# Four casts of two bias rows, made by ScalarE instead of VectorE

## The chip, the cores and the metric

The kernel runs on one core of a Trainium2 chip. The metric is the device time of one execution in microseconds (us), the median of several runs. The engines are TensorE (PE, and PEld for its weight loads), VectorE (DVE), ScalarE (ACT), GpSimd (POOL) and SyncE (SP, which issues most of the DMAs).

## The reference, cut to what matters

The input is four images of 64 x 64 positions with 96 channels. Two layers follow one another. The first normalizes each image, projects every position and runs a gated linear recurrence with 96 x 16 states along the 4096 positions of an image; it is most of the work. The second is attention without softmax and a feed forward layer whose numbers are rounded to small float formats:

```python
# q_mul rounds to fp8 (5 exponent bits, 2 mantissa bits), q_acc to fp16 (5, 10)
def _qlinear(x, W, b):
    y = q_acc(jnp.einsum('bsk,nk->bsn', q_mul(x), q_mul(W)))
    return q_acc(y + q_mul(b))
h = jax.nn.relu(_qlinear(x, W1, b1))     # 96 -> 384
y = _qlinear(h, W2, b2)                  # 384 -> 96
```

So the two biases, b1 of 384 numbers and b2 of 96, are rounded to fp8 once and then added as they are.

## The kernel before, in words

An image is cut into 8 chunks of 512 positions, 32 chunks in all. A chunk's recurrence is 12 tiles of 128 states by 512 positions, so there are K = 384 tiles, and the program is one loop over steps s from 0 to 383. In each step the engines get, in this order of issue: on TensorE the B matmuls of tile s + 3 (`b_proj`), the A matmuls of tile s + 1 (`a_proj`) and the C matmuls of tile s (`c_proj`), three each, all by the helper `project` (line 292); on ScalarE the copy of B with its bias into the buffer bu (`b_copy`, line 924) and the copy of the last state (`keep`, line 953); on GpSimd the product of bu of tile s + 2 (`b_mul`, line 927) and, for some tiles, the product of C (`c_mul_pool`, line 976); on VectorE the scan of tile s (`scan`, line 943), the product of A of tile s + 1 (`a_mul`, line 936), and for the other tiles the product of C (`c_mul`, line 967).

What is not part of a tile's own work is put behind that, at `call(s)`, from a table of steps written by hand: the projections of the next chunk, its norms, the sums over states, the attention and the feed forward layer of earlier chunks. Each engine works through its instructions in the order in which they were issued. The first steps and the part behind step 383 are ordered by a planner (`Plan`) that goes by the engines' costs that the code states.

PSUM banks: A has two, B one, C and D one each, and M three, which all side work shares in turn. The A bank of a tile is free again when its scan has read it, the B bank when `b_copy` has.

The weights of the second layer are prepared in steps far ahead of their use: `weights_attention`, `weights_ffn1`, `weights_ffn2` and `weights_bias` at steps 20, 32, 44 and 56 transpose them on TensorE, and the step after each writes them out of PSUM. For the biases that is `biases_out` in step 57: b1 from PSUM to fp8 (line 381) and back to f32 (line 382), then b2, loaded in full width by a DMA at the start, from SBUF to fp8 (line 384) and back to f32 (line 385). The readers of the results are `relu` and `relu_vector` (lines 1249 and 1260) and `bias_out` (line 1284), from 379 us on.

Of the kernel before, what the change touches and what calls it, by code (L numbers as in the profile page):

```python
# [13 lines left out]
AF = mybir.ActivationFunctionType  # L14
# [4 lines left out]
B, H, W, C = 4, 64, 64, 96  # L19
# [15 lines left out]
NK = HID // P  # L35
# [21 lines left out]
APPLY_DVE = (2, 6)  # L57
QUANT_POOL = (1, 3, 4, 5)
BIAS_DVE = (0, 2, 3, 4, 5, 7)
TOTAL_DVE = (0, 2, 3, 4, 5)  # L60
ON_POOL = (0, 2, 9)
AT0 = {
# [19 lines left out]
def conv_attn_hybrid_kernel(  # L82
# [19 lines left out]
    nc = tc.nc  # L102
# [21 lines left out]
    def sb(tag, shape, dtype, name):  # L124
        pool = big if tag in ("x", "gx", "z", "rep") else work
        return pool.tile(shape, dtype, tag=tag, name=name, bufs=BUFS[tag])
# [128 lines left out]
    b1_q = const.tile([P, NK], F32, name="b1_q")  # L255
    b2_q = const.tile([P, C], F32, name="b2_q")
# [3 lines left out]
    b2_sb = sb("y16", [P, C], F32, "b2_sb")  # L260
# [113 lines left out]
    def weights_bias():  # L374
        ps = bank("M", [P, NK], "b1_ps")
        nc.tensor.transpose(ps, b1_sb, ident[:NK, :NK])
        return lambda: biases_out(ps)

    def biases_out(ps):
        b1_8 = small.tile([P, NK], F8, tag="b1_8", name="b1_8", bufs=1)  # L380
        nc.vector.tensor_copy(b1_8, ps, saturate=False)
        nc.vector.tensor_copy(b1_q, b1_8)
        b2_8 = small.tile([P, C], F8, tag="b2_8", name="b2_8", bufs=1)
        nc.vector.tensor_copy(b2_8, b2_sb, saturate=False)
        nc.vector.tensor_copy(b2_q, b2_8)

    norms = {}

# [800 lines left out]
    def ffn(b, i, s0):  # L1189
        nm = f"{b}_{i}"  # L1190
        whole = s0 + max(AT["attention"], AT["residual_f"]) >= K
# [3 lines left out]
        v, ln = {}, LayerNorm(1e-5, f"f_{nm}", key)  # L1195
        t = xt[b, i]

        def tile_of(tag, drain_tag, shape, dtype, name):
            return sb(drain_tag if phase["end"] else tag, shape, dtype, f"{name}_{nm}")
# [32 lines left out]

        def quant_in():
            v["xq"] = tile_of("xq", "h", [C, TC], F8, "xq")
            nc.scalar.activation(v["xq"], v["ps"][0:C], AF.Copy, saturate=False)  # L1235

        def hidden(m):
            v["h", m] = bank("M", [P, TC], f"h_ps{m}_{nm}")
# [14 lines left out]
        def round_hidden(m):  # L1253
            if m == 0:
                v["h16"] = sb("rep", [P, NK, TC], F16, f"h16_{nm}")
            nc.scalar.copy(v["h16"][:, m, :], v["h", m])  # L1256

        def relu_vector(m):
            h = v["h16"][:, m, :]
# [32 lines left out]
        def store():  # L1292
# [6 lines left out]
            (("rstd_f", ln.rstd),),  # L1299
            (("apply_f", apply),),  # L1300
            (("transpose_f", transpose), ("quant_in", quant_in)),
            tuple((f"{f.__name__}{m}", f, m) for m in range(NK) for f in (hidden, relu)),
            (("project_f", project_out), ("round_out", round_out)),
# [17 lines left out]
        def job(engine, cost, fn, *args, **kw):  # L1321
            return None if fn in done else end.job(engine, cost, fn, *args, **kw)
# [9 lines left out]
        def finish(a, mv):  # L1332
            end.rank = END_RANKS[1] if b < B - 1 else END_RANKS[2] + END_PAIR[i]
            if vector:
                a = job("DVE", 0.96, apply, after=[a], take=[f"xn8:{nm}"], free=mv, late=0.1, port=True)
            elif whole:
                a = job("ACT", 1.45, apply, after=[a], take=[f"xn8:{nm}"], free=mv, late=0.1)
            if transpose not in done:
                a = job("PE", 0.25, transpose, after=[a], take=[f"C:{nm}"], free=[f"xn8:{nm}"], late=0.2)
                a = job("ACT", 0.49, quant_in, after=[a], take=[f"h:{nm}"], free=[f"C:{nm}"], late=0.1)  # L1340
            if hidden not in done:
                r, h, c = [], None, None
                for m in range(NK):
                    h = job("PE", 0.22, hidden, m, after=[a, h], take=[f"M:{m}{nm}"],
                            free=[f"h:{nm}"] if m == 2 else [], late=0.2)
                    c = job("ACT", 0.48, round_hidden, m, after=[h, c],
                            take=[f"rep:{nm}"] if m == 0 else [], free=[f"M:{m}{nm}"], late=0.1)
                    r.append(job("DVE", 0.27, relu_vector, m, after=[c], late=0.1, port=True))
                if i in QUANT_POOL:
                    a = job("POOL", 1.43, quant, after=r, take=[f"bu:q{nm}"], free=[f"rep:{nm}"], late=0.1, port=True)  # L1350
                else:
                    a = job("ACT", 1.38, quant, after=r, take=[f"bu:q{nm}"], free=[f"rep:{nm}"], late=0.1)
            a = job("PE", 0.5, project_out, after=[a], take=[f"A:y{nm}"], free=[f"bu:q{nm}"], late=0.2)
            a = job("ACT", 0.37, round_out, after=[a],
                    take=[f"xs:{nm}"], free=[f"A:y{nm}"], late=0.1)
            e = "DVE" if whole and i in BIAS_DVE else "POOL"
            a = job(e, 0.55 if e == "DVE" else 0.88, bias_out, e, after=[a], take=[f"xl:{nm}"], free=[f"xs:{nm}"], late=0.1, port=True)
            e = "DVE" if whole and i in TOTAL_DVE else "POOL"
            a = job(e, 0.5 if e == "DVE" else 0.88, total, e, after=[a], take=[f"z:{nm}"], free=[f"xl:{nm}"], late=0.1, port=True)
            job("SP", 0.5, store, after=[a], late=2.5, free=[f"z:{nm}"])  # L1360

        if whole:
            wholes[b, i] = begin, finish, ln
            return
        end.rank = END_RANKS[1]
        a = job("DVE", 0.48, residual)
        a = job("DVE", 1.04, stats, after=[a], take=[f"mv1:{nm}"], late=0.1)
        a = job("POOL", 1.3, ln.rstd, after=[a], late=0.1)
        if apply not in done:
            a = job("ACT", 1.45, apply, after=[a], take=[f"xn8:{nm}"], free=[f"mv1:{nm}"], late=0.1)  # L1370
        finish(a, [])

    wholes = {}
# [275 lines left out]
```

## Time and profile before

| what | value |
|---|---|
| median of 3 runs | 1141.15 us (1138.0 to 1142.48) |
| profiled execution: its own time | 1141.61 us |
| profiled execution: span from first to last instruction | 1139.9 us |
| granted TensorE clock, mean | 0.993 |
| instructions | 20132 |
| busy share: TensorE, VectorE, GpSimd, ScalarE | 96%, 96%, 90%, 79% |
| the four casts | once, from 190.93 to 192.51 us |

In the lines of a profile a group reads: line, engine, operation, output <- inputs by the program's names without numbers (so b1_q and b2_q are both b_q, b1_sb and b2_sb both b_sb, b1_8 and b2_8 just b), and shapes as partitions x elements. In a timeline each line begins with the start and the duration in us; what stands in brackets at its end is the idle time of that engine before it, and what ended that. In a view of waits the three numbers are the total in us, the number of waits and the longest. A release that the view names is the last event by its reckoning; where the engine it names had long been done, it was another.

### The profile page before, as it was taken

To read this page: it belongs to the slowest core of one execution; us is meant where nothing else is said; L and a number is where in the kernel's file an instruction comes from. 1 tells how busy PE (TensorE), PEld (TensorE's weight loads), DVE (VectorE), ACT (ScalarE), POOL (GpSimd) and SP (SyncE) were. 2 spreads that over 40 slices of the span, in tenths; PEclk is the share of its full clock that TensorE was granted. 3 is DMA by queue.
4 is the path that set the end of the run, shared out by engine and by line. 5 is a ranking of instruction groups with operands and counts; after the bars stand their busy time and mean duration, and the time that the engine had idled before them with its cause. 6 is when DMAs were issued, how large, how long until landed. Compare 5 with 4: busy or idle time off the path is not lost. (4 is left out here: it accounts for less than half of the span.)

```text
span 1139.9 us, 20132 instructions
## 1 busy us (share of the span) xinstructions
PE 1097.5 (96%) x5691; PEld 860.8 (76%) x5691; DVE 1089.5 (96%) x1874; ACT 904.5 (79%) x2448; POOL 1029.8 (90%) x1048
## 2 busy tenths in 40 slices
PE   6999999999999999999999999999999999999985
PEld 5677777777877777777778777777777777777663
DVE  6999999999999999999999999999999999999985
ACT  4587666766766988888898889889888888886577
POOL 5688999899999999999999999999999899999754
PEclk8999999999999999999999999999999999999999
DMA  7578988888888988988888888888898888797432
GB/s 185 129 155 166 193 175 167 172 190 174 183 183 170 190 179 177 180 180 188 175 185 191 185 181 184 172 173 186 178 181 181 170 182 178 166 186 165 91 91 56
DMA packets 98074, 193.62 MB, mean 170 GB/s; under 512 B 48509, under 2 KB 56641, under 8 KB 97962
## 3 DMA queue, kind: packets, MB, share of 16 engines
q0 software_dynamic: 17376, 91.63, 44.5%
q1 hardware_dynamic: 79996, 100.69, 35.3%
q8 instruction: 45, 0.74, 0.3%
q14 instruction: 67, 0.55, 0.1%
q10 hardware_dynamic: 590, 0.02, 0.0%
HBM read 20.36 MB, written 12.58 MB: 29 GB/s over the span
## 5 line engine op out<-in xcount | busy, mean ns | idle before, releaser
L927 POOL TENSOR_TENSOR bu<-bu,rep 128x512 f32<-128x512 f32 x384 | 596.0, 1587 | 13.8 <-ACT bu L924 6.5
L943 DVE TENSOR_TENSOR_SCAN h<-Aps,state,bu 128x512 f32<-128x512 f32 x336 | 427.1, 1271 | 7.7 <-POOL bu L927 3.4
L924 ACT ACTIVATE bu<-Bps,b_bac 128x512 f32<-128x512 f32 x384 | 262.8, 684 | 113.2 <-PE Bps L292 105.1
L936 DVE SCALAR_TENSOR_TENSOR Aps<-Aps,b_bac,rep 128x512 f32<-128x512 f32 x384 | 281.6, 734 | 4.5 <-PE Aps L292 4.2
L292 PE MATMUL Bps<-xs,w 128*128 128x512 f32 x768 | 265.7, 427 | 6.8 <-ACT bu L924 6.5
L292 PE MATMUL Aps<-xs,w 128*128 128x512 f32 x768 | 243.2, 397 | 1.4 <-DVE h L943 1.0
L292 PEld LDWEIGHTS Aps<-xs,w 128*128 128x128 f32 x768 | 142.1, 188 | 41.7 <-DVE h L943 9.0
L976 POOL TENSOR_TENSOR ch<-ch,h 128x512 f32<-128x512 f32 x94 | 151.3, 1610 | 3.9 <-ACT ch L973 3.8
L292 PEld LDWEIGHTS Bps<-xs,w 128*128 128x128 f32 x768 | 128.6, 190 | 31.1 <-ACT bu L924 14.2
L292 PE MATMUL Aps<-xl,w 128*128 128x512 f32 x384 | 151.7, 395 | 0.0
L292 PE MATMUL Bps<-xl,w 128*128 128x512 f32 x384 | 151.4, 394 | 0.0
L292 PE MATMUL Cps<-xs,w 128*128 128x512 f32 x384 | 120.6, 395 | 0.0
L292 PE MATMUL Dps<-xs,w 128*128 128x512 f32 x384 | 120.6, 395 | 0.0
L967 DVE SCALAR_TENSOR_TENSOR ch<-Dps,b_bac,h 128x512 f32<-128x512 f32 x161 | 119.3, 741 | 0.4 <-PE Dps L292 0.3
L983 POOL DMA_DIRECT2D ch<-ch x94 | 107.4, 1142 | 7.4 <-DMA ch<-ch 3.2
L967 DVE SCALAR_TENSOR_TENSOR ch<-Cps,b_bac,h 128x512 f32<-128x512 f32 x129 | 95.5, 740 | 0.0
L292 PEld LDWEIGHTS Bps<-xl,w 128*128 128x128 f32 x384 | 72.2, 188 | 17.7
L292 PEld LDWEIGHTS Aps<-xl,w 128*128 128x128 f32 x384 | 72.0, 188 | 17.7
L292 PEld LDWEIGHTS Cps<-xs,w 128*128 128x128 f32 x384 | 72.0, 188 | 17.6
L292 PEld LDWEIGHTS Dps<-xs,w 128*128 128x128 f32 x384 | 72.0, 188 | 17.6
L292 PE MATMUL Dps<-xl,w 128*128 128x512 f32 x192 | 75.7, 394 | 0.0
L292 PE MATMUL Cps<-xl,w 128*128 128x512 f32 x192 | 75.6, 394 | 0.0
(212 smaller groups left out, 2181.3 us busy)
## 6 DMA issues: line engine op xcount, KB each, us to landing
ch<-ch POOLq DMA_DIRECT2D x94, 768.0 KB, 6.7
rep<-dd SPq DMA_DIRECT2D x372, 128.0 KB, 4.0
ch<-ch POOLq DMA_DIRECT2D x30, 384.0 KB, 5.4
xl<-lo SPq DMA_DIRECT2D x62, 128.0 KB, 3.2
x<-in_x_dram SPq DMA_DIRECT2D x32, 192.0 KB, 3.2
xatd<-xat SPq DMA_DIRECT2D x32, 192.0 KB, 2.8
xal<-xatd SPq DMA_DIRECT2D x32, 192.0 KB, 4.4
out_dram<-o SPq DMA_DIRECT2D x32, 192.0 KB, 3.9
```

Source lines behind the costliest of these rows:

```text
L292: nc.tensor.matmul(ps, lhsT=wt[:, n], rhs=mv, start=(n == 0), stop=(n == 2))
L924: nc.scalar.activation(self.bu, self.b_ps, AF.Identity, bias=self.bias(0))
L927: nc.gpsimd.tensor_tensor(self.bu, self.bu, rep[self.b, self.i][:, self.cg, 1], ALU.mult)
L936: nc.vector.scalar_tensor_tensor(self.a_ps, self.a_ps, self.bias(1), rep[self.b, self.i][:, self.cg, 0], ALU.add, ALU.mult,)
L943: nc.vector.tensor_tensor_scan(self.h, self.a_ps, self.bu, 0.0 if self.i == 0 else state[self.sh, self.cg], ALU.mult, ALU.add,)
L967: nc.vector.scalar_tensor_tensor(self.slot(), self.c_ps, self.bias(2), self.h, ALU.add, ALU.mult)
L976: nc.gpsimd.tensor_tensor(self.ch, self.ch, self.h, ALU.mult)
L983: nc.gpsimd.dma_start(chs[g, base(g)], chs.pop((g, sh)), accum_op=ALU.add)
```

## The change

The four casts in `biases_out` are issued to ScalarE, as two activations with the function Copy into fp8 and two copies back to f32. Two tuples, both empty, are added at the top, and two places of the feed forward layer and of its planning ask whether a tile is in them; with the empty tuples they issue what they issued before.

```diff
+QIN_DVE = ()
+ROUND_DVE = ()
...
     def biases_out(ps):
         b1_8 = small.tile([P, NK], F8, tag="b1_8", name="b1_8", bufs=1)
-        nc.vector.tensor_copy(b1_8, ps, saturate=False)
-        nc.vector.tensor_copy(b1_q, b1_8)
+        nc.scalar.activation(b1_8, ps, AF.Copy, saturate=False)
+        nc.scalar.copy(b1_q, b1_8)
         b2_8 = small.tile([P, C], F8, tag="b2_8", name="b2_8", bufs=1)
-        nc.vector.tensor_copy(b2_8, b2_sb, saturate=False)
-        nc.vector.tensor_copy(b2_q, b2_8)
+        nc.scalar.activation(b2_8, b2_sb, AF.Copy, saturate=False)
+        nc.scalar.copy(b2_q, b2_8)
...
         def quant_in():
             v["xq"] = tile_of("xq", "h", [C, TC], F8, "xq")
-            nc.scalar.activation(v["xq"], v["ps"][0:C], AF.Copy, saturate=False)
+            if whole and i in QIN_DVE:
+                nc.vector.tensor_copy(v["xq"], v["ps"][0:C], saturate=False)
+            else:
+                nc.scalar.activation(v["xq"], v["ps"][0:C], AF.Copy, saturate=False)
...
-            nc.scalar.copy(v["h16"][:, m, :], v["h", m])
+            if whole and NK * i + m in ROUND_DVE:
+                nc.vector.tensor_copy(v["h16"][:, m, :], v["h", m])
+            else:
+                nc.scalar.copy(v["h16"][:, m, :], v["h", m])
...
-                a = job("ACT", 0.49, quant_in, after=[a], take=[f"h:{nm}"], free=[f"C:{nm}"], late=0.1)
+                e = "DVE" if whole and i in QIN_DVE else "ACT"
+                a = job(e, 0.6 if e == "DVE" else 0.49, quant_in, after=[a], take=[f"h:{nm}"], free=[f"C:{nm}"], late=0.1)
...
-                    c = job("ACT", 0.48, round_hidden, m, after=[h, c],
+                    e = "DVE" if whole and NK * i + m in ROUND_DVE else "ACT"
+                    c = job(e, 0.6 if e == "DVE" else 0.48, round_hidden, m, after=[h, c],
```

## The prediction

> **What bounds the kernel now.** I read the page from the top: engine shares first, then the 40 slices, then the chain.
>
> ```profile
> PE 1097.5 (96%) x5691; PEld 860.8 (76%) x5691; DVE 1089.5 (96%) x1874; ACT 904.5 (79%) x2448; POOL 1029.8 (90%) x1048
> DVE  6999999999999999999999999999999999999985
> ACT  4587666766766988888898889889888888886577
> ```
>
> VectorE (DVE) is busy 90% or more of nearly every slice, with TensorE (PE) level with it, so time taken from VectorE can count; ScalarE (ACT) has slack in the early slices, where the four casts run. The chain that ended last is of no use here: followed back from the end it covers only the last 65 us, from 1075 us on, and the casts run near 191 us. So the question is local, and I go to the timeline of each engine around the casts. First VectorE (start, duration, line, operation, idle before it in brackets):
>
> ```profile
> 187.67 1.28 DVE L943 TENSOR_TENSOR_SCAN h<-Aps,state,bu 128x512 f32<-128x512 f32 x1
> 189.56 0.76 DVE L936 SCALAR_TENSOR_TENSOR Aps<-Aps,b_bac,rep 128x512 f32<-128x512 f32 x1 [0.61 <-PE Aps L292]
> 190.26 0.75 DVE L967 SCALAR_TENSOR_TENSOR ch<-Dps,b_bac,h 128x512 f32<-128x512 f32 x1
> 190.93 0.15 DVE L381 CAST b<-b_ps 128x3 fp8e5<-128x3 f32 x1
> 191.12 1.13 DVE L382 CAST b_q<-b 128x3 f32<-128x3 fp8e5 x1
> 192.16 0.20 DVE L384 CAST b<-b_sb 128x96 fp8e5<-128x96 f32 x1
> 192.39 0.21 DVE L385 CAST b_q<-b 128x96 f32<-128x96 fp8e5 x1
> 192.51 1.27 DVE L943 TENSOR_TENSOR_SCAN h<-Aps,state,bu 128x512 f32<-128x512 f32 x1
> ```
>
> The reader is to see two things. The casts run once in the whole kernel and take VectorE from 190.93 to 192.51 us, 1.58 us from the end of the multiply to the next scan. And one of them, three elements wide, takes 1.13 us where its like takes 0.15. GpSimd's (POOL's) timeline over the same stretch says why:
>
> ```profile
> 188.77 2.20 POOL L927 TENSOR_TENSOR bu<-bu,rep 128x512 f32<-128x512 f32 x1
> 190.02 2.19 POOL L976 TENSOR_TENSOR ch<-ch,h 128x512 f32<-128x512 f32 x1
> 191.27 1.11 POOL L676 TENSOR_TENSOR gmv<-gt,gmc 96x1 f32<-96x1 f32 x1
> ```
>
> GpSimd's product of line 976 ends at 192.21 and the cast of line 382 at 192.25. Then ScalarE's timeline, where the casts go:
>
> ```profile
> 188.92 0.69 ACT L924 ACTIVATE bu<-Bps,b_bac 128x512 f32<-128x512 f32 x1
> 189.51 0.18 ACT L953 COPY state<-h 128x1 f32<-128x1 f32 x1
> 191.02 0.69 ACT L924 ACTIVATE bu<-Bps,b_bac 128x512 f32<-128x512 f32 x1 [1.33 <-POOL bu L927]
> 191.61 0.18 ACT L953 COPY state<-h 128x1 f32<-128x1 f32 x1
> 193.76 0.69 ACT L924 ACTIVATE bu<-Bps,b_bac 128x512 f32<-128x512 f32 x1 [1.97 <-PE Bps L292]
> ```
>
> ScalarE idles 1.33 us and then 1.97 us. The view names GpSimd for the first gap, but the copy at 191.02 also needs the third B matmul, which ended at 190.92 (start 190.53, 0.39 long): that is what it waited for.
>
> **What the Trainium skill says.** "SBUF — State Buffer", section "Who interferes with whom": VectorE and GpSimd share a port pair under an exclusive lock that is held for a whole instruction; copies and casts from SBUF to SBUF can enter the mode that takes it, and the loser blocks. The trace agrees as far as it can: line 382 (SBUF to SBUF) takes 1.13 us and ends with GpSimd's product, line 381 (from PSUM, as narrow) 0.15. The same section gives ScalarE ports of its own, so I expect no such stall there; no run shows these casts on it. "ScalarE: Activation LUTs", section "What ACT_TABLE_LOAD costs": an ACTIVATE with immediates takes 186 ns + 0.833 ns an element, and neighbours overlap by about 93 ns. The trace's nearest rows are near it: 128x1 copies 182 ns, 128x4 activations with immediates 189 to 206 ns, 97x97 copies from PSUM 232 to 236 ns, 128x96 activations 274 ns. The trace has a single ACT_TABLE_LOAD, of 1283 ns, although Sigmoid, Copy, Identity, Square and Relu follow it, so these casts bring no second one.
>
> **The change part by part.**
>
> *Taken from VectorE: four casts.* Busy 0.15 + 1.13 + 0.20 + 0.21 = 1.69 us; what counts is the pitch, 1.58 us. Can the scan of tile 58 start at 190.93 instead of 192.51? Its A operand is the multiply at 189.56, done by 190.32. Its bu is GpSimd's product of tile 58, started at 186.54 and done by 188.75 (product 59 is issued in step 57, just ahead of the product of C for tile 56, so product 58 is one earlier). Both are there: the whole 1.58 us is exposed on VectorE.
>
> *Can the neighbours follow?* The next A multiply (tile 59) needs matmuls that end at 191.62; VectorE would reach it at 190.93 + 1.19 = 192.12. The C product of tile 58 needs matmuls ending near 192.32; reached at 192.77. The scan of 59 needs bu at 190.97; reached at 193.42. The A multiply of 60 needs an A bank that the scan of 58 frees at about 192.2; TensorE could then issue it at 193.5, when its B matmuls are issued, not at 193.84, and end near 194.4; VectorE comes at 194.61. So no new wait follows in the next steps, and the lead is carried.
>
> *How much of it survives.* In the stretch after the casts the waits of TensorE's weight loads are VectorE's doing:
>
> ```profile
> PEld Aps L292 <- DVE h L943: 3.3, 6, 0.6
> ```
>
> That is the view of waits from 192 to 257 us: six waits, 3.3 us in all. Of them the matmul stream itself loses about 0.34, 0.29, 0.28, 0.2 and 0.2 us by 211 us (each start against the previous start plus the 0.235 us at which unstalled matmuls follow one another), and another 0.34 at 242.5: some 1.3, then 1.65 us, that TensorE can gain once VectorE comes earlier. VectorE's first idle time after the casts is at 247.16 us, 0.17 us, for TensorE's A matmuls. Until then VectorE never waits, so it keeps up to 1.58 us; from there TensorE's lead is what counts, 1.3 to 1.6. Later releasers (GpSimd's bu at 339 us, 0.53; the chain of the gram matrix at 344 us, 1.76 on TensorE) are issued behind the same engines and should come earlier with them, but part may be lost. I take **1.3 us** kept, with 0.2 and 1.6 as the ends.
>
> *Put on ScalarE: four casts.* They come behind the state copy of step 57 (ends 189.69) and ahead of the bu copy at 191.02. Their matmul ran at 186.88 and the bias row was loaded at 43 us, so neither is waited for. Price: two of 3 columns at 0.19 (rows of 128x4), two of 96 at 0.24 to 0.27 (the rows above) = 0.86 to 0.92 us; with the overlaps of the skill 0.64 (estimate); with a pause of 0.19 us ahead of three of them, as the one between the affine and the copy at 194.42 and 195.36, 1.5. The cover is the gap of 1.33 us, so 0 to 0.17 us stick out, and these meet the 1.97 us gap: the bu copy frees the one B bank, whose next matmul starts at 192.71, a full microsecond after it. Cost taken: 0. Without that cover TensorE's B matmuls would be late by whatever is over about 2.3 us.
>
> *Waits that change owner.* The first cast now gives the M bank back from ScalarE, near 189.9 instead of 191.1; its next tenant is the group sum at 192.59. The later readers of the two bias tiles wait for ScalarE instead of VectorE, from 379 us on, nearly 190 us after; nothing is queued behind that. No DMA and no queue of SP or GpSimd moves. GpSimd loses the rival for its port, worth at most its stretched line 676 (1.11 against 0.19 us), beside work that nobody waits for at once. The new branches name two empty tuples: the instructions they issue and the costs the end's planner sees are those of before. Cost 0.
>
> *Sum.* -1.3 + 0 + 0 = -1.3 us, so the profiled execution (1141.61 us, 1.71 of it outside the 1139.9 span) would come to 1140.3. That execution stands 0.46 us above the median of 1141.15, so the median goes to **1139.9 us**: 0.1%. The three runs before spread over 4.5 us, and a measurement of this kernel can tell about 0.5%, 5.7 us, from no change. So the answer is no change that can be told.
>
> **The rivals.**
>
> *The lead is swallowed.* A later wait that isn't VectorE's doing absorbs it. For: TensorE is as full as VectorE (33.00 of 33 us in the stretch from 355 to 388). Against: TensorE's own waits up to 242 us name VectorE. Gives 1141 us. Chance 0.20.
>
> *Slower: the casts delay the B bank.* B has one bank; what the four casts take beyond 2.3 us (the gap and the microsecond behind it) stops TensorE. It decides from 0.58 us a cast, three times the 128x4 row. At 0.75 each, 3.0 us, TensorE would be 0.7 us late and the bu stream behind it, and the lead is gone: 1141.9 us. For: no row shows a copy out of fp8 on ScalarE. Against: copies into fp8 there follow the usual price (598 ns for 512 columns). Chance 0.05.
>
> *Displaced transfers.* DMA engines are 81 to 87% busy in these stretches; 1.5 us of shift can change which transfer runs into which. The longest wait of GpSimd on a DMA is 1.7 us, so one collision costs 0.4 net (1141.6) or brings as much; for 5.7 us it would have to repeat four times or more. Chance 0.12, of which I put 0.10 beyond 0.5%, evenly to both sides.
>
> *The change does nothing*, if VectorE's scan waits at 190.93 for something this profile hides: 1141.15. It lies within the swallowed case.
>
> **How the numbers follow.** Gain kept 0.63, swallowed 0.20, displaced 0.12, slower 0.05. Beyond 0.5% on either side: 0.05 each from displaced transfers, and 0.01 each for a fault in the others. So faster 0.06, within 0.88, slower 0.06. The range takes the kept gain's ends (1139.6 to 1141.0), the slow rival's 1141.9, and the spread of medians that runs of 1138.0 to 1142.5 allow: 1136.9 to 1143.0.
>
> **What would show it.** Right: VectorE's timeline has no cast near 191 and the scan follows the multiply within 0.05 us; ScalarE shows four casts of 0.18 to 0.28 us between a state copy and a bu copy that starts no later than 191.3; the wait of TensorE on line 943 next after it is shorter. VectorE busy falls by some 1.7 us, ScalarE's grows by 0.9. Wrong: a bu copy later than 192, casts over 0.5 us, a table load beside them, or a median more than 5.7 us off.

## The result, and the profile after

| | before | after |
|---|---|---|
| median of 22 runs each | 1141.6 us | 1139.12 us |
| ratio after to before, 95% interval | | 0.998 (0.9973 to 0.9986) |
| profiled execution, span | 1139.9 us | 1135.9 us |

That is 2.3 us less (1.6 to 3.1). The sign is the one forecast, 1139.12 us lies within the range of 1136.9 to 1143.0, and the change is smaller than 0.5%. It is more than the 1.3 us of the sum, and it can be told from no change after all: with 22 runs each the interval leaves 1 out. The page of the changed kernel is nearly the same; VectorE has lost 1.3 us of busy time and four instructions, ScalarE has gained the four:

```profile
PE 1097.0 (97%) x5691; PEld 862.4 (76%) x5691; DVE 1088.2 (96%) x1870; ACT 904.8 (80%) x2452; POOL 1029.3 (91%) x1048
```

VectorE's timeline of the changed kernel at the casts' old place:

```profile
187.81 1.28 DVE L945 TENSOR_TENSOR_SCAN h<-Aps,state,bu 128x512 f32<-128x512 f32 x1
189.71 0.76 DVE L938 SCALAR_TENSOR_TENSOR Aps<-Aps,b_bac,rep 128x512 f32<-128x512 f32 x1 [0.61 <-PE Aps L294]
190.41 0.75 DVE L969 SCALAR_TENSOR_TENSOR ch<-Dps,b_bac,h 128x512 f32<-128x512 f32 x1
191.07 1.27 DVE L945 TENSOR_TENSOR_SCAN h<-Aps,state,bu 128x512 f32<-128x512 f32 x1
...
194.76 0.73 DVE L938 SCALAR_TENSOR_TENSOR Aps<-Aps,b_bac,rep 128x512 f32<-128x512 f32 x1
```

This execution runs 0.15 us later than the one before up to here (189.71 against 189.56). The multiply of line 969 is followed by the scan at once: from one scan to the next it takes 191.07 - 187.81 = 3.26 us, where it took 192.51 - 187.67 = 4.84. That is 1.58 us less, and no idle time opens in the steps that follow. ScalarE's timeline of the changed kernel:

```profile
189.66 0.18 ACT L955 COPY state<-h 128x1 f32<-128x1 f32 x1
189.73 0.18 ACT L383 ACTIVATE b<-b_ps 128x3 fp8e5<-128x3 f32 x1
189.94 0.19 ACT L384 CAST b_q<-b 128x3 f32<-128x3 fp8e5 x1
190.04 0.28 ACT L386 ACTIVATE b<-b_sb 128x96 fp8e5<-128x96 f32 x1
190.35 0.27 ACT L387 CAST b_q<-b 128x96 f32<-128x96 fp8e5 x1
191.17 0.69 ACT L926 ACTIVATE bu<-Bps,b_bac 128x512 f32<-128x512 f32 x1 [0.54 <-POOL bu L929]
```

The casts take 0.89 us from the first start to the last end, the gap of 1.33 us has shrunk to 0.54, and the bu copy starts at 191.17, which with the 0.15 us taken off is the 191.02 of before. Nothing on ScalarE is late.

**Where the rest of the time is.** The scans can be followed through the whole kernel: I took the start of each of the 384 scans in one trace and subtracted that in another. In the changed kernel they stand 0.14 us later than in the first profile of before ahead of the casts, 1.44 us earlier right behind them (a step of 1.58), still 1.44 us earlier at 336 us (tile 113), and 3.84 earlier at the last scan. So 1.58 us come at the casts, none is lost in the nearly 150 us that follow, and another 2.4 us appear past 336 us, where none of the moved casts runs and only the readers of their results do. (The expectations below call this place 345 us; on the axis of the timelines shown here the scans begin to part between 336 and 339 us.)

### The profile page after: what moved, and what is told of

Read it like the earlier page. It is cut to its first block, busy times and chain, and to the rows that moved or that the text cites. A ratio compares the mean times of both kernels' runs of the same rounds, so it can differ in the third digit from the quotient of the medians.

```text
span 1135.9 us, 20132 instructions
## 1 busy us (share of the span) xinstructions
PE 1097.0 (97%) x5691; PEld 862.4 (76%) x5691; DVE 1088.2 (96%) x1870; ACT 904.8 (80%) x2452; POOL 1029.3 (91%) x1048
```

## The experiments

"Lead" is what the scans gain on the first profile of before between tile 57 and the place named; a lead below zero is a delay. The kernels ran in three sessions, each against runs of the kernel before in the same session.

| kernel | lead behind the casts (us) | further, 336 us to the last scan (us) | ratio to before (95%) |
|---|---|---|---|
| after | 1.58 | 2.40 | 0.998 (0.9973 to 0.9986) |
| before again | 0.01 | 2.35 | 1.0007 (0.9999 to 1.0015) |
| after again | 1.57 | 1.48 | 0.9979 (0.9972 to 0.9986) |
| weight casts too | 1.59 | 1.43 | 0.998 (0.9973 to 0.9987) |
| 32 statistics more | -3.55 | 3.29 | 1.0023 (1.0013 to 1.0033) |
| b1 alone | 0.13 | 1.89 | 0.9994 (0.9984 to 1.0004) |
| b2 alone | 0.37 | 1.58 | 0.999 (0.9977 to 1.0002) |
| b2, and b1 from PSUM | 1.45 | 0.32 | 0.9984 (0.9978 to 0.9991) |
| casts on both engines | 0.07 | 1.00 | 0.9995 (0.9987 to 1.0003) |
| casts put back | -0.01 | -0.54 | 1.0006 (0.9997 to 1.0015) |
| matrix copies too | 1.57 | 2.02 | 0.9979 (0.9972 to 0.9987) |
| casts six times | -1.74 | 1.97 | 1.0023 (1.0011 to 1.0035) |

Up to 336 us the lead stays within 0.1 us of the first column, but for two kernels: "b2, and b1 from PSUM" has 1.27 left from tile 71 on, and "casts six times" ends at -1.95.

**Is the further lead real?** The kernel before was run again, and the changed one.

> The kernel before, run once more as a measure of scatter; every theory expects a ratio of 1.000 with an interval that shows how fine a comparison of five rounds is. Its profile set against the first one of the same program shows how far two executions drift apart: the theory that the lead past 345 us is scatter expects the start of the scans to differ by steps of 0.3 to 1 us of either sign after 345 us and by less than 0.1 us before; the theory that the change also gains something there expects the two to lie together within 0.3 us.

The second profile of the same program keeps within 0.04 us of the first one from tile 57 to 336 us and then runs away from it by 2.35 us, in steps of up to 0.9 us of both signs. The first step is 0.61 us, at the scan of tile 114, which is the wait at 339 us that the prediction named. In the first profile VectorE and GpSimd have there:

```profile
339.36 1.28 DVE L943 TENSOR_TENSOR_SCAN h<-Aps,state,bu 128x512 f32<-128x512 f32 x1 [0.53 <-POOL bu L927]
337.10 0.90 POOL L987 DMA_DIRECT2D ch<-ch  x1 [1.72 <-DMA ch<-ch]
```

In the second profile GpSimd waits 0.96 us for its transfer, and VectorE not at all:

```profile
336.26 0.90 POOL L987 DMA_DIRECT2D ch<-ch  x1 [0.96 <-DMA ch<-ch]
```

The changed kernel waits 0.90 us at this place, and run again 1.82, so the wait does not go with the change. The 2.4 us past 336 us are what two executions of one program can differ by, and the first profile of before was the slower one there. For what the two profiles show, the scatter theory holds.

> The changed kernel once more, in the same session as the others. The theory of the pitch (all of the gain is the 1.6 us that VectorE no longer spends near 191 us) expects 1.3 to 1.6 us under the kernel before, ratio 0.9986 to 0.9989. The theory that something downstream gains too (the lead seen at the end of the scans was 4.0 us) expects 2.3 to 4 us, ratio 0.9965 to 0.998.

The ratio is 0.9979, 2.4 us less (1.6 to 3.2); the local lead is 1.57 again. By this run alone the theories cannot be told apart: the ratio is one that the second expects, and the 1.6 us of the first are the edge of the interval. The two measurements of the changed kernel together leave the first less room: 2.35 us, give or take 0.55 (an estimate from the two intervals, as if the sessions were independent), some 0.8 us more than the lead. The question is taken up again below.

**Which part of the change pays?** The halves were made alone.

```diff
 # b1 alone
-        nc.scalar.activation(b2_8, b2_sb, AF.Copy, saturate=False)
-        nc.scalar.copy(b2_q, b2_8)
+        nc.vector.tensor_copy(b2_8, b2_sb, saturate=False)
+        nc.vector.tensor_copy(b2_q, b2_8)
```

> Only the two casts of b1 on ScalarE; the two of b2 stay on VectorE. In the kernel before, the four hold VectorE for 1.58 us, of which the second cast of b1 has 1.0 us beyond its like. The theory that this 1.0 us is a wait for GpSimd's product on the shared port: the first cast of b2, also SBUF to SBUF, now comes first and waits in its place until about 192.2 us, so VectorE is held for 1.3 to 1.5 us still and gains only 0.1 to 0.3. The rival that the 1.0 us belongs to that one instruction (three columns, or out of fp8): the casts of b2 take 0.35 to 0.4 us and the gain is 1.2 us.

VectorE's timeline of that kernel, and GpSimd's:

```profile
190.55 0.75 DVE L969 SCALAR_TENSOR_TENSOR ch<-Dps,b_bac,h 128x512 f32<-128x512 f32 x1
191.22 1.31 DVE L386 CAST b<-b_sb 128x96 fp8e5<-128x96 f32 x1
192.56 0.21 DVE L387 CAST b_q<-b 128x96 f32<-128x96 fp8e5 x1
192.69 1.28 DVE L945 TENSOR_TENSOR_SCAN h<-Aps,state,bu 128x512 f32<-128x512 f32 x1
```

```profile
190.31 2.14 POOL L978 TENSOR_TENSOR ch<-ch,h 128x512 f32<-128x512 f32 x1
```

The slow instruction of before is gone, and the next one has become slow in its place: the first cast of b2, 0.20 us in the kernel before, takes 1.31 us and ends at 192.53, as GpSimd's product does at 192.45. Taking two of the four casts away brings 0.13 us. The rival that the time belonged to the b1 instruction is out.

> Only the two casts of b2 on ScalarE; those of b1 stay on VectorE. Both theories: the second cast of b1 still takes 1.1 us and VectorE is held for 1.2 to 1.3 us, a gain of 0.3 to 0.4. With the port theory the two halves of the change together bring 0.4 to 0.7 us of the 1.58.

For b2 alone the edit is the other half. The second cast of b1 takes 1.13 us as before, and VectorE is held for 1.22 us, from 191.90 to the scan; the lead is 0.37 us:

```profile
192.08 1.13 DVE L384 CAST b_q<-b 128x3 f32<-128x3 fp8e5 x1
193.12 1.27 DVE L945 TENSOR_TENSOR_SCAN h<-Aps,state,bu 128x512 f32<-128x512 f32 x1
```

The halves bring 0.13 + 0.37 = 0.50 us, the whole 1.58: the 1.1 us between them is paid as long as either pair stays there, each of which has a copy from SBUF to SBUF.

```diff
 # b2 alone, and b1's second copy out of PSUM
-        nc.vector.tensor_copy(b1_q, b1_8)
+        nc.vector.tensor_copy(b1_q, ps)
```

> As the run before (b2 on ScalarE, b1 on VectorE), but b1's second copy reads PSUM instead of the fp8 tile, so that neither copy goes from SBUF to SBUF; the rounding of b1 to fp8 is left out of the values by that. Port theory: both copies take about 0.15 us, VectorE is held for 0.3 to 0.4 us and gains 1.2 to 1.3 us of the 1.58 with as many instructions as in the run before. The rival that the second instruction of three columns is slow for itself, or waits for the first: 1.1 us still.

VectorE's timeline:

```profile
191.32 0.15 DVE L383 CAST b<-b_ps 128x3 fp8e5<-128x3 f32 x1
191.39 0.15 DVE L384 COPY b_q<-b_ps 128x3 f32<-128x3 f32 x1
191.45 1.28 DVE L945 TENSOR_TENSOR_SCAN h<-Aps,state,bu 128x512 f32<-128x512 f32 x1
```

With as many instructions as for b2 alone, on the same engine, VectorE is held for 0.13 us instead of 1.22, a lead of 1.45. What changed is where the second copy reads. With that it also no longer reads fp8 and no longer depends on the copy ahead of it, but in the b1-alone run a cast out of f32 with no copy ahead of it waited all the same. So the wait belongs to the first copy from SBUF to SBUF that comes. That GpSimd is what it waits for rests on the ends: in four kernels that have the wait, the copy ends at 192.25, 192.53, 193.21 and 192.06 us and GpSimd's product at 192.21, 192.45, 193.17 and 192.03 (before, b1 alone, b2 alone, casts on both engines). No kernel took that product away.

**Does the change do anything beside?**

```diff
 # casts on both engines: the four of VectorE again, into tiles d1_8, d1_q, d2_8, d2_q
+        nc.vector.tensor_copy(d1_8, ps, saturate=False)
+        nc.vector.tensor_copy(d1_q, d1_8)
+        nc.vector.tensor_copy(d2_8, b2_sb, saturate=False)
+        nc.vector.tensor_copy(d2_q, d2_8)
```

> The changed kernel, with the four casts made on VectorE as well (into tiles that nothing reads). ScalarE's part of the change without VectorE's. The theory of the pitch: VectorE is held for 1.58 us again, no scan differs from the kernel before by more than 0.1 us until 345 us, ratio 1.000; the casts on ScalarE cost nothing. The theory that the change gains something else (less waiting of later readers, some 0.7 us): ratio 0.9994. The rival that ScalarE's casts cost: scans later than before by what sticks out of ScalarE's gap.

The scans lie within 0.08 us of the kernel before up to 336 us: ScalarE's four casts cost nothing. The ratio of 0.9995 has both 1.000 and 0.9994 in its interval, so a further gain by ScalarE's part is not ruled out.

> The changed program text with the four casts put back on VectorE. On all five engines it issues the instructions and waits of the kernel before, so the theory of the pitch expects 1.000, and what it differs by is the scatter between two loads of one program. So far seven kernels built from the changed text lie 0.5 to 1.0 us below what their scans' lead explains; the theory that this text carries a further gain expects 0.9994 or less here.

The lead is -0.01 us and the ratio 1.0006 (0.9997 to 1.0015). The interval leaves out 0.9994, so the program text alone carries no gain of 0.7 us. This run and before again issue the instructions of the kernel before and lie 0.7 and 0.8 us above it; both intervals have 1.000 in them, so that much can be scatter. It does not explain the excess of 0.7 us, of the measured 2.3 over the lead of 1.58. Ratio and lead at 336 us set side by side, all nine kernels with at least two of the casts on ScalarE, made once, lie 0.5 to 1.0 us below what their lead explains; scatter alone would be expected to put some of them above. "Casts six times" lies 0.7 above. The cause stays open.

**Is VectorE's time paid one for one?**

```diff
+        st = small.tile([P, J, 6], F32, tag="dose", name="dose", bufs=1)
+        for n in range(32):
+            nc.vector.bn_stats(st[:, n % J, :], b2_sb)
```

> The changed kernel with 32 statistics instructions (128x96, result unused) added on VectorE behind the casts' place in step 57; in this kernel such ones follow one another at 0.185 us, so VectorE is held up for 5.9 us. The theory that VectorE's time at this place is paid one for one: 5.9 us over the changed kernel at the end, about 4.3 over the kernel before, ratio 1.0038. If a delay there is partly swallowed later: under 3 us over before, ratio under 1.0026. If a delay is amplified downstream, as the 4.0 us between the two profiles for a pitch of 1.6 would have it: 8 us or more over before, ratio 1.007.

The 32 statistics take VectorE 5.12 us (191.35 to 196.47), 0.16 us each and not 0.185. The scans fall 3.55 us behind, and 5.12 - 1.58 is 3.54. In time the kernel lies at 1.0023 against 0.9979 for the changed kernel of the same session: 5.0 us for 5.12. By the two intervals that is 3.6 to 6.4 us (an estimate). Against the kernel before the time is 2.6 us (1.5 to 3.8), which by itself falls under the 3 us that I had set for a partly swallowed delay; but the dose was smaller than planned, and paid one for one it makes 3.5 us, which the interval holds. The scans decide up to 336 us: they are 3.57 us behind there still, so nothing is swallowed up to that place. An amplified delay, 8 us or more, is out.

**Is it so at other places?** Two kernels put more one-off copies on ScalarE.

```diff
 # weight casts too
-        return lambda: nc.vector.tensor_copy(w_qt[0:C, :], ps)
+        return lambda: nc.scalar.copy(w_qt[0:C, :], ps)
...
-        return lambda: nc.vector.tensor_copy(w1_q, ps, saturate=False)
+        return lambda: nc.scalar.activation(w1_q, ps, AF.Copy, saturate=False)
...
-        return lambda: nc.vector.tensor_copy(w2_q, ps, saturate=False)
+        return lambda: nc.scalar.activation(w2_q, ps, AF.Copy, saturate=False)
```

> The changed kernel with the three other one-off casts of weights (96x97, 96x384 and 128x288, out of PSUM, near 95, 127 and 159 us) on ScalarE too. They hold VectorE for 0.17 + 0.46 + 0.36 = 0.99 us there, and ScalarE has gaps of 1.3 us or more where they would land. The theory of the pitch: each scan that follows comes earlier by its pitch, the scan at 191 us about 1.0 us earlier than in the changed kernel, and the time falls by another 0.7 to 1.0 us, ratio to before 0.9975 to 0.998. The theory that leads are swallowed: the scans come earlier there, but the lead is back to that of the changed kernel by 345 us. A rival on ScalarE: a cast of 0.5 us there delays a bu copy and a scan waits; no gain.

The expectation fell for two of the three. Against the changed kernel the scans gain 0.17 us at tile 22 and keep it; they gain 0.44 us at tile 34 and have lost it at tile 38; they gain 0.36 at tile 46 and have lost it at tile 50. TensorE's timeline of this kernel shows what takes the lead:

```profile
133.79 0.74 PE L294 MATMUL Bps<-xs,w 128*128 128x512 f32 x2 [0.65 <-ACT bu L926]
165.81 0.73 PE L294 MATMUL Bps<-xs,w 128*128 128x512 f32 x2 [0.64 <-ACT bu L926]
```

The changed kernel has the same waits at 133.94 and 165.96 us, of 0.64 us each. That is 0.15 us later, and the two executions lie 0.13 us apart at tile 57 anyway: a few steps behind both casts TensorE waits for ScalarE's copy out of the one B bank, and goes on no earlier than when VectorE had no lead. That this wait takes the lead is read from its place; no run removed it. In the changed kernel the next such wait behind the bias casts stands at 232.38 us, 41 us on, and the lead passes it whole. In time the kernel is equal to the changed one.

```diff
+        copy = nc.scalar.copy if s0 < K else nc.vector.tensor_copy
...
-            nc.vector.tensor_copy(v["gk"], v["ps"])
+            copy(v["gk"], v["ps"])
```

The same was done for `kvff`, `rmat` and, for all images at once, `w_qt`.

> The changed kernel with one more weight copy (96x97, near 95 us) and, for the first three images, three of the four copies of the attention's chain of small matrices on ScalarE, nine copies of about 97x96 out of PSUM. Each holds VectorE for about 0.17 us. If what VectorE is spared is always gained: 10 times 0.17 = 1.7 us less than the changed kernel, ratio to before 0.9965. If a lead lasts only where no chain over ScalarE and TensorE follows (as with two of the weight casts, whose lead was gone four tiles later): 0.2 us from the first copy and less than half of the others, ratio 0.9975 to 0.998. If ScalarE is late with a copy, the matrix chain stops TensorE: ratio at 0.998 or above.

The ratio is 0.9979, as for the changed kernel again. Against that kernel the scans gain 0.17 us at tile 22; around the second image's chain they gain 0.33 us up to tile 217 and have lost it at tile 218. VectorE's timeline there, of this kernel and then of the changed kernel again:

```profile
622.15 0.56 DVE L1055 TENSOR_TENSOR x<-o_ps,x 128x384 f32<-128x384 f32 x1 [0.71 <-PE o_ps L1050]
```

```profile
622.77 0.56 DVE L1055 TENSOR_TENSOR x<-o_ps,x 128x384 f32<-128x384 f32 x1 [0.38 <-PE o_ps L1050]
```

What VectorE was spared it waits longer for TensorE's output projection: 0.71 instead of 0.38 us. The second branch of the expectation held: the first copy's lead lasts, and the lead at this chain is gone by the end of it. Neither kernel is a better version.

**When would ScalarE be too late?**

```diff
+        for _ in range(6):
             nc.scalar.activation(b1_8, ps, AF.Copy, saturate=False)
             nc.scalar.copy(b1_q, b1_8)
             nc.scalar.activation(b2_8, b2_sb, AF.Copy, saturate=False)
             nc.scalar.copy(b2_q, b2_8)
```

> The changed kernel with its four casts on ScalarE made six times over: 24 instead of 4. They follow one another at 0.89 us a set, 5.3 us in all, against a gap of 1.44 us and a microsecond of room for the B bank behind it. The price that the prediction gave for late casts: TensorE's next B matmuls 2.9 us later than in the changed kernel, the scans 2.5 to 2.7 us later, so about 1.0 us behind the kernel before at 221 us and 2.6 us above the changed kernel in time, ratio to before 1.000 to 1.001. If ScalarE had room for more (or the buffers of bu hid it): under 1 us. If every us on ScalarE were paid: 4.4 us above the changed kernel.

TensorE's timeline, VectorE's, and the table by stretch of TensorE's granted clock (length, then busy time and instructions of PE, PEld, DVE, ACT, POOL, then clock, DMA share, GB/s):

```profile
194.72 0.30 PE L686 MATMUL gm_ps<-gmv,third 96*96 96x1 f32 x2 [1.09 <-ACT b L385]
195.93 0.73 PE L294 MATMUL Bps<-xs,w 128*128 128x512 f32 x2 [0.91 <-ACT bu L927]
```

```profile
197.63 0.76 DVE L939 SCALAR_TENSOR_TENSOR Aps<-Aps,b_bac,rep 128x512 f32<-128x512 f32 x1 [2.06 <-PE Aps L294]
198.91 0.75 DVE L970 SCALAR_TENSOR_TENSOR ch<-Dps,b_bac,h 128x512 f32<-128x512 f32 x1 [0.52 <-PE Dps L294]
```

```profile
194.00:196.00 2.00, 0.37 (x3) 0.31 (x3) 1.57 (x2) 1.86 (x9) 1.01 (x2) 1.00 0.65 180
198.00:200.00 2.00, 2.00 (x7) 1.51 (x6) 1.48 (x3) 0.99 (x2) 2.00 (x3) 0.50 0.74 150
```

The chain is the one named: the bu copy is late, TensorE's B matmuls wait for it, VectorE waits for the A matmuls. Counted from the start of tile 57's C product (190.41 in the changed kernel, 191.14 here) the B matmuls start after 4.79 us instead of 2.44, 2.35 later and not 2.9. A set follows the set ahead at 0.79 us and not at 0.89, so the six end after 4.82 us and not 5.3; that is the half microsecond by which the price was too high. But the scans end up 3.3 us behind those of the changed kernel a few tiles on (a lead of -1.74 against 1.58), and 3.5 at 336 us, not 2.5 to 2.7. The ratio, 1.0023 (1.0011 to 1.0035), lies above the 1.000 to 1.001 expected, and the time is 5.0 us above the changed kernel's by the ratios of two sessions. I had left out that TensorE runs at half its clock for a while after these stops: VectorE waits another 0.52 us for the matmuls of its next product and 0.42 for those of the next tile. The repeated casts also held the M bank, which stopped TensorE for 1.09 us by itself; so this kernel may overdraw the price of late casts. From the intervals the time cannot decide between 3.3 and 4.4 us.

## Why the prediction was right, point by point

- *What VectorE loses, 1.58 us.* Right, to the hundredth: the step between the scans of tiles 57 and 58.
- *Why one cast took 1.13 us.* Right as far as the runs go. The wait on the port that VectorE shares with GpSimd was argued from two end times and a section of the Trainium skill. The three kernels with halves and with PSUM show that the wait goes with a copy from SBUF to SBUF; that it lasts until GpSimd's product ends is seen in four executions, and the port itself in none. What I did not say is that it can't be had in parts: 0.13 and 0.37 us for the halves.
- *The neighbours can follow.* Right: the A matmuls of tile 60 start at 193.64 with no wait, VectorE takes them at 194.76 with none.
- *How much survives.* The mis-sized term. I put 1.3 us, from the time TensorE could gain; 1.57 to 1.58 us were still there at 336 us. My own count had reached 1.65 us for TensorE by 242.5 us, enough to carry all of the 1.58. The idle time at 247 us that I feared would take a part is there in the changed kernel again, at 245.58 us, and 0.17 us long as before: TensorE had come along entirely.
- *ScalarE's cost, 0.* Right: 0.18, 0.19, 0.28 and 0.27 us, 0.92 together against 0.86 to 0.92 priced and 0.89 from the first start to the last end, in a gap of 1.33, and no scan moved when they were added alone. The estimate of 0.64 with the skill's overlaps was too low: the third starts 0.10 us behind the second, but the second and the fourth, which read what the one ahead wrote, start 0.21 and 0.31 us behind it and do not overlap it.
- *GpSimd's line 676.* Wrong in the reading: I took its 1.11 us for time lost to VectorE. Without the casts the same instruction (now line 678) takes 1.07: it starts before the product ahead of it ends, and the casts had not stretched it.
- *Busy time.* I expected VectorE's to fall by some 1.7 us and ScalarE's to grow by 0.9; the pages show 1.3 and 0.3. These sums also differ by 0.3 us each between the two profiles of before, so they are a poor measure here.
- *The sum.* 1.3 us forecast, 1.58 shown by the scans, 2.3 (1.6 to 3.1) by the time. The mechanism accounts for the 1.58 us and not for all of the 2.3: the 0.7 us over the lead were not traced to anything. The text of the changed kernel without the moved casts does not have them, and nine kernels with casts on ScalarE all do. That this is scatter was not shown, nor is a gain by ScalarE's part past 336 us, where the readers of the two bias tiles run; the prediction put that at nothing.
- *What can be told.* Too coarse: I held that a measurement cannot tell less than 5.7 us from no change, beside a spread of 4.5 us over three runs. The interval over 22 runs each is 1.5 us wide.
- *The rivals.* The swallowed lead did not happen here, but leads of 0.3 to 0.4 us were lost at three other places, each at a wait over ScalarE or TensorE a few steps on. The slow rival's chain is real and begins where ScalarE's room ends, at some 2.5 us (4.82 less the 2.35 that TensorE was late; 2.3 predicted); the casts use 0.89. Displaced transfers: past 336 us two executions of one program part in steps of up to 0.9 us, of both signs, the first of them behind a wait of GpSimd for a transfer; nothing ties them to the change.

## What to carry to other kernels

A small copy from SBUF to SBUF on VectorE can cost many times what its like costs (1.13 us against 0.15 here) where GpSimd is busy, and the wait passes to the next such copy if only one is removed: look for a cast that ends with a GpSimd instruction, and move all of them or read from PSUM. Whether the time spared counts depends here on the waits that follow: where VectorE's next idle time was 55 us off and TensorE was waiting for it, all of it lasted; where a wait over another engine stood a few steps on, it was lost. For a gain of a thousandth follow the starts of one recurring instruction through two traces, and run the same program twice, before anything past the edit is put down to it.

## What the runs showed of the hardware

TensorE's granted clock fell to half after short stops. In the kernel with the dose it waited 3.72 us for VectorE, and soon after going on its matmuls followed one another at about 0.43 us instead of 0.235, with a granted clock of 0.50 from 200 to 202 us; there it cost nothing, since VectorE was behind anyway:

```profile
197.79 0.73 PE L294 MATMUL Aps<-xs,w 128*128 128x512 f32 x2 [3.72 <-DVE h L948]
200.00:202.00 2.00, 2.00 (x6) 1.52 (x5) 2.00 (x4) 0.87 (x4) 0.00 (x0) 0.50 0.53 104
```

In the kernel with six sets of casts it was stopped twice, for 1.09 and 0.91 us, and the clock fell to 0.50 from 198 to 200 us. In the changed kernel, without such stops, it is 1.00 in every stretch from 186 to 208 us. The Trainium skill, "TensorE: Matmul & The Clock Gate", section "What's actually happening", describes a gate that halves the clock when the engine has been idle for a window of about 3.4 us. The 3.72 us agree with that; in the second case 2.0 us of idle time, broken by a small matmul, were enough.
